# Depthwise 3x3 taps as diagonal matmuls, value copies on another engine, and a new set of due times

## The chip, the cores and the metric

The kernel runs on one core of a Trainium2 chip. A core has five engines that run their own instruction queues side by side: TensorE (PE in the profile), which multiplies matrices and writes to the accumulators (PSUM); VectorE (DVE); ScalarE (ACT); GpSimd (POOL); and SyncE (SP), which here only issues transfers. DMA engines move data between the chip's memory and the core's. The metric is the device time of one execution in microseconds (us). Before the change, three runs took 5207.44, 5217.47 and 5219.44 us: the median is 5217.47.

## What is computed

The input is a batch of 8 images of 256 channels and 32x32 pixels, fp32. Four layers follow, each adding a function of the group-normalised input to its input:

```
x = x + L0(gn(x))   # attention, 8 heads of 64, q and k normalised
x = x + L1(gn(x))   # 3x3 convolution, 256 -> 256 channels
x = x + L2(gn(x))   # 3x3 convolution, 256 -> 256 channels
x = x + L3(gn(x))   # the mixer, below
```

The mixer (layer 3), cut to its steps:

```
xn = layernorm(xs, norm_w, norm_b)
xm = mamba_v(four groups of 64 channels of xn) + skip_scale * xc      # selective scans over 1024 tokens
g  = sigmoid(conv1d(conv1d(x_concat, qdw), qpw));  xg = g * xm
R  = conv1d(conv1d(xg, rdw, groups=C), rpw) + xg
xm2 = conv1d(conv1d(concat(xs, R), fdw, groups=2C), fpw) + xs
x_local  = conv1d(xm2, lc_w, groups=C)
x_global = mha(xm2, 8 heads of 32)
x_out = gelu(layernorm(concat(x_local, x_global) @ fc_w.T + fc_b))
xi = ln_hw(x_out as image)
xi = conv2d(xi, dwc_w, 3x3, padding 1, feature_group_count=C) + dwc_b   # depthwise: one 3x3 filter a channel
out = layernorm(xi, norm_w, norm_b) @ proj_w.T + proj_b
```

The line with `dwc_w` is the one whose work moves: each pixel of a channel is the sum of nine neighbours, each with its own weight.

## The kernel before

Tiles have 128 channels (partitions) by 1024 pixels; an image is two such halves, t = 0 and 1. The whole program is first recorded, operation by operation, in streams: for each image b, `A` (layer 0's attention), `O` (its output projection), `C` (both convolutions), `N` (the load and norm ahead of the scans), `F0` to `F3` (what each of the four scans needs), `S` (the scan steps), `Z0` to `Z3` (what follows each scan), `B` (mixer up to its attention and with it) and `E` (the mixer's back end). `V` makes the convolutions' weights once.

A planner then writes the order of every engine out by hand. The table `PACE` has, for each stream and image, four due times between which the stream's operations are spread (`rank`, line 489); `arrange` (line 522) goes through them by a model of the engines, picks among the operations that could begin earliest the one with the lowest rank, and each engine is given its instructions in that fixed order. So an engine that waits at an instruction holds up all that stands behind it. Due times matter only by the order in which they put operations. An operation that needs nothing but constants (`fetches`, line 459) is due no earlier than its first user.

Buffers come from pools, and the planner gives a pool's tiles out in turn: `wsp` has 6 tiles `w` of 128x512 for weights, which ACT's queue loads (`chunk`, line 831); `ps_big` has 2 accumulator tiles `big` of 128x1024; `ps_cv` 2 and `ps_acc` 1 of 128x512; `hsp` 4 tiles `hs` of 128x1024 for the scans; `vp` one tile `v`, shared by the values of layer 0's attention and the mixer's.

What the steps of the prediction touch:

- *The scan* (`scan_steps`, line 1674) has 64 units an image. A unit is, on DVE, `hs <- du*bc` (drive), two scans `hs <- da, hs` whose decays `da` ACT makes, and `hs <- hs*bc` (weigh). After each pair of units PE adds up: four matmuls `y <- hs, sel`. These free the two `hs` tiles. 
- *Around the scan*: `branch_front` (line 1587) has the matmuls `raw,w`, `u,w_mxpw` and `u,mdtw`; `branch_back` (line 1649) has `xm,w_minw` and `u,w_moutw`, and the addition that ends `xm`.
- *The mixer up to its attention* (`back_layers`, line 1958): matmuls `xm,qdw`, then `q,qpr`, the gate, `rd,w`, `fd,w`, and `x`; then `mixer_attention` (line 1818). Its values tile has, for each of 8 heads, 32 columns of values and 32 of ones (the ones give the softmax sums). DVE fills the ones with a memset over 128x2048 elements and copies the values from the accumulator twice (128x1024 each).
- *The back end* (`back_out`, line 2114, and `back_end`, line 2129): a projection into `room[0]` and `room[1]`; a layer norm, which has 16 pairs of one-column matmuls (`mean_w`), a chain of 12 small DVE instructions (the inverse root) and 8 matmuls `ident,ln_r`; a GELU; statistics of each channel; then per half one activation that normalises `xo[t]`, one that makes the centre tap, and eight `scalar_tensor_tensor` on DVE, one for each other tap. Half 1 of the result goes to `room[0]`, the tile that half 0 of the input is in. A second layer norm (first `room,mean_w`, 4 matmuls, then as above) and the projection `room,w` (8 matmuls) end the image.

The tap loop of a half:

```
scalar.activation(dw[t], xo[t], AF.Identity, bias=col("dwc_b", t), scale=col("dwc_w", 9 * t + 4))
for k in (0, 1, 2, 3, 5, 6, 7, 8):
    rows, from_rows = inside(k // 3 - 1)
    at, from_at = inside(k % 3 - 1)
    vector.scalar_tensor_tensor(acc[:, rows, at], src[:, from_rows, from_at],
        col("dwc_w", 9 * t + k), acc[:, rows, at], ALU.mult, ALU.add)
```

Every instruction goes through one recording line, so the profile gives all of them line 252; they are told apart by their tiles' names. An fp32 matmul shows as two records of PE and two of PEld (its weight loads).

Of the kernel before, what the change touches and what calls it, by code (L numbers as in the profile page):

```python
# [36 lines left out]
OUT_OF_TURN = {("ps_big", "big")}  # L37
PACE = {
    "A": (
        (415, 603, 929, 929),  # L40
        (1475, 1542, 1636, 1677),
        (1977, 2062, 2145, 2236),
        (2549, 2617, 2690, 2765),
        (3076, 3147, 3224, 3283),
        (3606, 3674, 3747, 3821),
        (4137, 4220, 4311, 4396),
        (4656, 4723, 4796, 4870),
    ),
    "B": (
        (2311, 2384, 2458, 2526),  # L50
        (2865, 2923, 2982, 3036),
        (3355, 3425, 3503, 3574),
        (3852, 3881, 4047, 4098),
        (4408, 4491, 4580, 4659),
        (4945, 5041, 5139, 5255),
        (5504, 5504, 5512, 5512),
        (6342, 6379, 6547, 6547),
    ),
    "C": (
        (1149, 1194, 1496, 1509),  # L60
        (1208, 1832, 1921, 2046),
        (2224, 2341, 2469, 2597),
        (2762, 2875, 3002, 3127),
        (3255, 3395, 3538, 3671),
        (3884, 3987, 4058, 4187),
        (4323, 4456, 4598, 4744),
        (4735, 4944, 5116, 5233),
    ),
    "E": (
        (2525, 2566, 2613, 2646),  # L70
        (3084, 3103, 3136, 3171),
        (3588, 3631, 3669, 3706),
        (4120, 4150, 4198, 4218),
        (4644, 4694, 4725, 4759),
        (5008, 5022, 5022, 5044),
        (5557, 5647, 5741, 5758),
        (5720, 5815, 5874, 5959),
    ),
    "F0": (
        (1525, 1563, 1607, 1611),  # L80
        (1772, 1776, 1816, 1954),
        (1459, 1509, 1529, 1529),
        (1904, 2029, 2038, 2039),
        (2248, 2334, 2334, 2334),
        (2815, 2815, 2904, 2904),
        (3595, 3601, 3609, 3609),
        (3315, 3520, 3761, 3761),
    ),
    "F1": (
        (1577, 1590, 1645, 1653),  # L90
        (2262, 2311, 2312, 2316),
        (2734, 2754, 2782, 2817),
        (3328, 3348, 3375, 3411),
        (3776, 3788, 3814, 3856),
        (4420, 4421, 4428, 4443),
        (4824, 4844, 4869, 4884),
        (5274, 5355, 5414, 5468),
    ),
    "F2": (
        (1730, 1776, 1802, 1811),  # L100
        (2088, 2268, 2292, 2387),
        (2836, 2854, 2873, 2921),
        (3363, 3396, 3401, 3411),
        (3922, 3927, 3928, 3958),
        (4159, 4364, 4376, 4487),
        (4918, 4945, 4994, 4997),
        (5538, 5541, 5541, 5558),
    ),
    "F3": (
        (1920, 1924, 1930, 1993),  # L110
        (2476, 2476, 2480, 2525),
        (3002, 3013, 3022, 3041),
        (3501, 3501, 3502, 3598),
        (4012, 4030, 4080, 4100),
        (4622, 4624, 4692, 4692),
        (5082, 5106, 5106, 5106),
        (5660, 5662, 5662, 5666),
    ),
    "N": (
        (1199, 1199, 1199, 1199),  # L120
        (2025, 2026, 2048, 2106),
        (2336, 2342, 2408, 2423),
        (2960, 3081, 3112, 3112),
        (3129, 3130, 3174, 3174),
        (3403, 3699, 3729, 3736),
        (4640, 4640, 4690, 4740),
        (4647, 4673, 4674, 4771),
    ),
    "O": (
        (1255, 1264, 1264, 1264),  # L130
        (1734, 1735, 1744, 1774),
        (2235, 2283, 2300, 2310),
        (2777, 2777, 2779, 2779),
        (3324, 3339, 3359, 3361),
        (3834, 3866, 3866, 3874),
        (4391, 4425, 4425, 4425),
        (4897, 4897, 4897, 4922),
    ),
    "S": (
        (1620, 1839, 2008, 2139),  # L140
        (2183, 2391, 2531, 2706),
        (2703, 2914, 3059, 3230),
        (3221, 3433, 3574, 3750),
        (3759, 3977, 4120, 4292),
        (4299, 4511, 4647, 4810),
        (4819, 5033, 5203, 5349),
        (5830, 5830, 5853, 5853),
    ),
    "V": (
        (1265, 1502, 1519, 1531),  # L150
    ),
    "Z0": (
        (1761, 1774, 1792, 1798),
        (2279, 2279, 2306, 2312),
        (2808, 2830, 2853, 2868),
        (3347, 3358, 3565, 3568),
        (3887, 3898, 3921, 3944),
        (4101, 4114, 4136, 4235),
        (4933, 4933, 4973, 4986),
        (5530, 5535, 5536, 5543),  # L160
    ),
    "Z1": (
        (1730, 1768, 1774, 1842),
        (2364, 2382, 2385, 2439),
        (2873, 2924, 2956, 2972),
        (3404, 3437, 3450, 3491),
        (3995, 4009, 4040, 4052),
        (4490, 4501, 4528, 4570),
        (5033, 5038, 5045, 5091),
        (5550, 5559, 5561, 5561),  # L170
    ),
    "Z2": (
        (1943, 1944, 1944, 1951),
        (2535, 2535, 2539, 2556),
        (3047, 3047, 3048, 3052),
        (3557, 3557, 3562, 3575),
        (4149, 4149, 4151, 4157),
        (4515, 4515, 4518, 4561),
        (5153, 5154, 5154, 5166),
        (5902, 5902, 5902, 5902),  # L180
    ),
    "Z3": (
        (2042, 2074, 2103, 2103),
        (2667, 2697, 2699, 2704),
        (3215, 3238, 3340, 3345),
        (3746, 3746, 3765, 3798),
        (4287, 4299, 4306, 4312),
        (4806, 4806, 4806, 4809),
        (5266, 5280, 5394, 5394),
        (5760, 5760, 5862, 5862),  # L190
    ),
    "H": (
        (-1268, -1255, -985, -985),
        (-819, -819, -762, -762),
        (-1453, -1453, -1438, -1185),
        (-657, -469, -357, -354),
        (-155, -155, -155, -155),
        (213, 213, 437, 463),
        (244, 542, 565, 602),
        (714, 714, 733, 843),  # L200
    ),
}

# [255 lines left out]
def appraise(ops, groups, rooms):  # L459
    for g in groups:  # L460
        op = ops[g.ops[0]]
        g.locks, g.bytes = locks(op), 0.0
        if g.tiles and all(region(a)[0] not in rooms or in_dram(a) for a in op["ins"]):
            if op["name"] == "dma_start" and in_dram(op["ins"][0]):
                g.fetches = not in_dram(op["outs"][0])
            elif op["name"] == "memset":
                g.fetches = True
        if g.engine:
            g.holds, g.takes = cost(op)
            if op["name"] == "dma_start":  # L470
                g.queue = True
                g.bytes = 4 * max(
                    int(np.prod([k for _, k in a.ap])) for a in op["outs"] + op["ins"]
                )
            elif g.engine == 2:
                g.table = TABLES.get(op["func"], 7)
            continue
        g.holds, beside = 0.0, set()
        for op in (ops[n] for n in g.ops):
            n = elements(op["outs"][0])  # L480
            if op["array"] != (P, P) and n > P and beside and op["at"] not in beside:
                beside.add(op["at"])
                continue
            beside = {op["at"]}
            g.holds += max(n / 0.6, 215 if g.holds else 135) + STAGGER[op["array"]]
        g.takes = g.holds + 165
# [262 lines left out]
def preact_stack(ctx: ExitStack, tc: tile.TileContext, I, out, cols):  # L749
# [1068 lines left out]
    def mixer_attention(x2, img, exact=False):  # L1818


        v = vp.tile([P, NKT, 8, 64], F32, tag="v", name="v3")
        vector.memset(v[:, :, :, 32:64], 1.0)
        wv = chunk("ainv", 0)
        for kt in range(0, NKT, 4):
            ps = big_tile()
            for i in range(4):
                for c in range(2):
# [4 lines left out]
                        start=c == 0,  # L1832
                        stop=c == 1,
                    )
            vector.tensor_copy(
                v[:, kt : kt + 4, :, 0:32],
                ps.rearrange("p (k a b) -> p k a b", k=4, b=32),
            )
# [285 lines left out]
    def inside(shift):  # L2124

        at = slice(max(0, -shift), 32 - max(0, shift))
        return at, slice(at.start + shift, at.stop + shift)

    def back_end(img, out_b):
        xo = room[0:2]  # L2130
        sq = [room[2], work("ln_sq")[:, 0:N]]
# [17 lines left out]
        for t in range(2):  # L2149
# [4 lines left out]
                bias=shift[:, t : t + 1],  # L2154
                scale=rs[:, t : t + 1],
            )
            src, acc = image(xo[t]), image(dw[t])
            scalar.activation(
                dw[t],
                xo[t],  # L2160
                AF.Identity,
                bias=col("dwc_b", t),
                scale=col("dwc_w", 9 * t + 4),
            )
            for k in (0, 1, 2, 3, 5, 6, 7, 8):
                rows, from_rows = inside(k // 3 - 1)
                at, from_at = inside(k % 3 - 1)
                vector.scalar_tensor_tensor(
                    acc[:, rows, at],
                    src[:, from_rows, from_at],  # L2170
                    col("dwc_w", 9 * t + k),
                    acc[:, rows, at],
                    ALU.mult,
                    ALU.add,
                )
        sq = [room[1], work("ln_sq")[:, 0:N]]
        layer_norm(dw, sq, WHOLE, big_tile, affine("norm_w", "norm_b"))

# [173 lines left out]
```

## Time and profile before

| what | value |
|---|---|
| runs before (us) | 5207.44, 5217.47, 5219.44 |
| median | 5217.47 |
| the profiled execution's own time | 5205.82 |
| its span, first to last instruction | 5204.1 |
| mean granted clock of TensorE | 0.941 |
| PE, DVE, ACT, POOL busy | 4700.7, 4115.6, 2880.8, 3.3 |
| DMA read and written | 483.18 MB, 63.18 MB |

The profile is one execution. "Busy" is the time in which an engine had at least one instruction at work. A granted clock of 1.00 is TensorE's full speed; at 0.50 it works at half. In a row of a group of instructions stand the engine, the operation, the tiles written and read, the shape, the count, then the busy time in us and the mean of one in ns, and last the idle time of the engine just before them with what ended it. In a timeline a row begins with its start and length in us. [...]

The longest chain of work through the span goes through PE for 64% of it and through DVE for 23%; the matmuls that write the `big` tile alone take 36% of it, and the scan's `hs` instructions on DVE 13%.

### The profile page before, as it was taken

The page shows a single profiled execution, that of the slowest core. Times are in us where ns is not written, and L with a number is a line of the kernel's source. Part 1 is how long each engine was busy: PE and PEld are TensorE (multiplying, and loading weights), DVE is VectorE, ACT ScalarE, POOL GpSimd, SP SyncE. Part 2 cuts the span into 40 slices and gives each one's busy share as a digit, 9 for nine tenths or more (in the row PEclk, how much of TensorE's full clock was granted, in tenths as well). Part 3 has the DMA queues.
Part 4 walks back from the last instruction along what each step waited for, and adds up shares of the span by engine and source line. Part 5 has one row for each costly group of instructions (what it writes and reads, how often), then busy time and mean ns, then how long its engine had stood idle before and what let it go on. Part 6 is the DMA issues. An engine that isn't in the chain of part 4 may idle for free.

```text
span 5204.1 us, 53545 instructions
## 1 busy us (share of the span) xinstructions
PE 4700.7 (90%) x18998; PEld 1917.1 (37%) x18998; DVE 4115.6 (79%) x5650; ACT 2880.8 (55%) x3768; POOL 3.3 (0%) x18
## 2 busy tenths in 40 slices
PE   8999879989999999999999999999999899698595
PEld 3363243243432534244442444325343343232222
DVE  3335989888888968979897788888877989999903
ACT  4426445646665565646666555655656556566342
POOL 0000000000000000000000000000000000000000
PEclk9999889999999999999999999899999999798696
DMA  4133344344343433433423343324433444344100
GB/s 134 46 100 110 121 151 127 95 125 134 106 125 101 144 100 108 126 102 126 131 91 107 106 142 125 112 74 141 123 109 108 125 131 157 98 126 126 66 18 23
DMA packets 256658, 575.15 MB, mean 111 GB/s; under 512 B 51192, under 2 KB 79224, under 8 KB 256384
## 3 DMA queue, kind: packets, MB, share of 16 engines
q1 hardware_dynamic: 167680, 431.11, 26.5%
q10 hardware_dynamic: 88704, 140.55, 8.8%
q8 instruction: 152, 2.49, 0.2%
q14 instruction: 122, 1.00, 0.1%
HBM read 483.18 MB, written 63.18 MB: 105 GB/s over the span
## 4 chain that ended last, share of the span: by engine, by line
PE 64%; DVE 23%; ACT 5%; issue 4%; DMA 3%; SPq 1%; DVEq 0%; ACTq 0%
PE big L252 36%; PE cv L252 14%; DVE hs L252 13%; PE acc L252 12%; PE y L252 2%; ACT p L252 2%; DVE room L252 2%; DMA rs<-inv 1%; DVE xt L252 1%; DVE u L252 1%; DVE st L252 1%; DVE xm L252 1%; SPq L252 1%; DVE p L252 1%; ACT taps L252 1%
## 5 line engine op out<-in xcount | busy, mean ns | idle before, releaser
L252 ACT ACTIVATE p<-big 128x1024 f32<-128x1024 f32 x1024 | 1013.4, 1019 | 556.1 <-PE big L252 487.7
L252 ACT ACTIVATE da<-dt,a_neg 128x512 f32<-128x512 f32 x1024 | 727.8, 720 | 721.6 <-DVE hs L252 584.8
L252 PE MATMUL acc<-p,v 128*64 128x512 f32 x3072 | 827.8, 622 | 31.3 <-ACT p L252 28.3
L252 PE MATMUL cv<-taps,w 128*128 128x256 f32 x3072 | 746.0, 393 | 40.3 <-DVE taps L252 29.4
L252 PEld LDWEIGHTS cv<-taps,w 128*128 128x128 f32 x3072 | 580.3, 194 | 295.6 <-issue 147.2
L252 DVE TENSOR_TENSOR hs<-du,bc 128x1024 f32<-128x1024 f32 x512 | 613.4, 1210 | 73.7 <-PE y L252 61.1
L252 DVE TENSOR_TENSOR_SCAN hs<-da,carry,hs 128x512 f32<-128x512 f32 x512 | 638.1, 1271 | 9.1 <-ACT da L252 8.2
L252 DVE TENSOR_TENSOR hs<-hs,bc 128x1024 f32<-128x1024 f32 x512 | 621.7, 1214 | 18.2 <-ACT carry L252 16.6
L252 PE MATMUL big<-q,k 64*128 64x512 f32 x2048 | 586.3, 654 | 31.3 <-ACT p L252 23.0
L252 DVE TENSOR_TENSOR_SCAN hs<-da,hs 128x512 f32<-128x512 f32 x512 | 608.9, 1210 | 5.0 <-ACT da L252 3.5
L252 DVE TENSOR_TENSOR p<-p 128x1024 f32<-128x1024 f32 x256 | 311.8, 1218 | 227.6 <-ACT p L252 164.7
L252 PE MATMUL y<-hs,sel 128*32 128x512 f32 x2048 | 336.9, 643 | 121.2 <-DVE hs L252 119.3
L252 PEld LDWEIGHTS acc<-p,v 128*64 128x64 f32 x3072 | 161.3, 136 | 590.7 <-issue 415.7
L252 PEld LDWEIGHTS big<-q,k 64*128 64x128 f32 x2048 | 160.3, 189 | 427.7 <-issue 207.7
L252 PE MATMUL big<-qk,qk 32*128 32x512 f32 x2048 | 298.1, 645 | 3.1 <-ACT qk L252 2.2
L252 PE MATMUL cv<-p,v 128*64 128x512 f32 x1024 | 276.9, 612 | 0.0
L252 PE MATMUL big<-xn,w 128*128 128x512 f32 x512 | 232.8, 600 | 2.8 <-ACT v L252 2.5
L252 PE MATMUL big<-o,w 128*128 128x512 f32 x384 | 182.5, 621 | 12.5 <-DVE o L252 12.2
L252 PEld LDWEIGHTS y<-hs,sel 128*32 128x32 f32 x2048 | 50.1, 111 | 337.8 <-DVE hs L252 187.6
L252 DVE SCALAR_TENSOR_TENSOR room<-room,vec,room 128x992 f32<-128x992 f32 (+1 forms) x128 | 156.7, 1224 | 10.0 <-ACT room L252 9.2
L252 PEld LDWEIGHTS big<-qk,qk 32*128 32x128 f32 x2048 | 82.3, 184 | 187.2 <-issue 140.1
L252 PEld LDWEIGHTS big<-xn,w 128*128 128x128 f32 x512 | 94.0, 190 | 130.0 <-issue 115.2
(234 smaller groups left out, 5038.5 us busy)
## 6 DMA issues: line engine op xcount, KB each, us to landing
bc<-bc SPq DMA_DIRECT2D x256, 512.0 KB
w<-wc ACTq DMA_DIRECT2D x384, 256.0 KB
dt<-dt_m SPq DMA_DIRECT2D x128, 512.0 KB
du<-du_m SPq DMA_DIRECT2D x128, 512.0 KB
rs<-inv SPq DMA_DIRECT2D x64, 256.0 KB
raw<-xm SPq DMA_DIRECT2D x64, 256.0 KB
dt_m<-dt SPq DMA_DIRECT2D x128, 128.0 KB
du_m<-a SPq DMA_DIRECT2D x128, 128.0 KB
```

Source lines behind the costliest of these rows:

```text
L252: made = op["call"](*args, **kwargs).ins
```

## The change

Five things change.

1. In `back_end`, the depthwise taps of images 5 and 6 (both halves) and of half 1 of image 7 are done by TensorE. ACT makes nine diagonal matrices of 128x128 for a half, `ident` scaled by the tap's weight of each channel, in three `w` tiles; 18 matmuls (nine taps, two halves of 16 rows, cut at the image's edge) add up in a `big` tile; ACT brings the sum out with the bias. The other images, and half 0 of image 7, keep the loop on DVE.
2. The mixer's memset of ones goes from DVE to POOL.
3. The mixer's values are copied out of the accumulator by ACT, not by DVE.
4. An activation that reads only constants counts as a fetch, so that the diagonals are due no earlier than their first user.
5. All numbers of `PACE` are set anew. The row `H` is used by no stream, before or after.

```diff
 PACE = {
     "A": (
-        (415, 603, 929, 929),
-        (1475, 1542, 1636, 1677),
...
+        (-682, -424, -117, -25),
+        (516, 618, 694, 732),
...
     "E": (
...
-        (5008, 5022, 5022, 5044),
-        (5557, 5647, 5741, 5758),
-        (5720, 5815, 5874, 5959),
+        (3976, 3978, 4015, 4017),
+        (4691, 4842, 5048, 5087),
+        (4451, 4453, 4775, 4871),
...
     "S": (
...
-        (4819, 5033, 5203, 5349),
-        (5830, 5830, 5853, 5853),
+        (3878, 4092, 4264, 4402),
+        (4841, 4852, 4853, 4853),
...
-            elif op["name"] == "memset":
+            elif op["name"] in ("memset", "activation"):
                 g.fetches = True
...
-        vector.memset(v[:, :, :, 32:64], 1.0)
+        pool.memset(v[:, :, :, 32:64], 1.0)
...
-            vector.tensor_copy(
+            scalar.copy(
                 v[:, kt : kt + 4, :, 0:32],
                 ps.rearrange("p (k a b) -> p k a b", k=4, b=32),
             )
...
+    def shifts():
+        for k in (4, 0, 1, 2, 3, 5, 6, 7, 8):
+            yield (k, *inside(k // 3 - 1), *inside(k % 3 - 1))
+
+    def taps_on_vector(x, dw, t):
...
+    def taps_on_array(x, dw, t):
+
+        diagonals = []
+        for n, (k, *_) in enumerate(shifts()):
+            if n % 4 == 0:
+                w = wsp.tile([P, HALF], F32, tag="w", name="w")
+            diagonals.append(w[:, (n % 4) * P : (n % 4 + 1) * P])
+            scalar.activation(
+                diagonals[n], ident, AF.Copy, scale=col("dwc_w", 9 * t + k)
+            )
+        src, ps = image(x), big_tile()
+        acc = image(ps)
+        for n, (k, rows, from_rows, at, from_at) in enumerate(shifts()):
+            for half in range(2):
+                first, last = max(rows.start, half * 16), min(rows.stop, half * 16 + 16)
+                shift = from_rows.start - rows.start
+                tensor.matmul(
+                    acc[:, first:last, at],
+                    diagonals[n],
+                    src[:, first + shift : last + shift, from_at],
+                    start=n == 0,
+                    stop=n == 8,
+                )
+        scalar.activation(dw, ps, AF.Identity, bias=col("dwc_b", t))
...
-            src, acc = image(xo[t]), image(dw[t])
...
+            if img["at"] in (5, 6) or (img["at"], t) == (7, 1):
+                taps_on_array(xo[t], dw[t], t)
+            else:
+                taps_on_vector(xo[t], dw[t], t)
```

`taps_on_vector` is the loop shown above, as a function.

## The prediction

> **What bounds the kernel now.** The page first: shares, then where in the span they hold.
>
> ```profile
> PE 4700.7 (90%) x18998; PEld 1917.1 (37%) x18998; DVE 4115.6 (79%) x5650; ACT 2880.8 (55%) x3768; POOL 3.3 (0%) x18
> ...
> PE   8999879989999999999999999999999899698595
> ...
> DVE  3335989888888968979897788888877989999903
> ...
> PEclk9999889999999999999999999899999999798696
> ```
>
> PE is near full for 34 slices of 130 us; in the last six it is not, while DVE is. So two regimes: PE bounds the first 4400 us, with 285 us idle in all (4400 less PE's busy time in 22 windows of 200 us); the tail is bound by something else. Stage windows of the tail (start:end, length, then PE, PEld, DVE, ACT, POOL busy, granted clock, DMA share, GB/s):
>
> ```profile
> 4400.00:4480.00 80.00, 60.13 (x233) 27.04 (x232) 75.19 (x108) 45.12 (x53) 0.00 (x0) 0.80 0.43 127
> 4480.00:4530.00 50.00, 29.18 (x79) 12.01 (x80) 48.49 (x45) 26.91 (x32) 0.00 (x0) 0.70 0.30 77
> 4530.00:4580.00 50.00, 41.61 (x102) 17.33 (x105) 45.67 (x63) 21.49 (x27) 0.00 (x0) 0.89 0.40 132
> 4580.00:4800.00 220.00, 188.71 (x839) 55.95 (x831) 218.13 (x198) 152.43 (x200) 0.00 (x0) 0.93 0.42 130
> 4800.00:4905.00 105.00, 47.54 (x147) 18.18 (x150) 102.60 (x119) 35.07 (x49) 0.00 (x0) 0.55 0.16 51
> ...
> 5100.00:5204.00 104.00, 51.67 (x152) 30.85 (x152) 41.20 (x70) 17.28 (x15) 0.00 (x0) 0.63 0.06 23
> ```
>
> From 4400 to 4905, where image 7's scan ends (its last y matmuls are at 4905), DVE works 490 of 505 us and PE 367. After it comes image 7's mixer, then its back end from 5100, a chain in which both engines wait for each other. What DVE does in 4400 to 4905 besides the scan, by groups of DVE instructions in that window:
>
> ```profile
> L252 DVE SCALAR_TENSOR_TENSOR room<-room,vec,room 128x992 f32<-128x992 f32 x16 | 19.8, 1238 | 0.1
> L252 DVE SCALAR_TENSOR_TENSOR room<-room,vec,room 128x961 f32<-128x961 f32 x16 | 19.3, 1208 | 3.7 <-ACT room L252 3.6
> ...
> L252 DVE MEMSET v<- 128x2048 f32 x2 | 3.5, 1765 | 0.8 <-issue 0.8
> ```
>
> These 32 multiply-adds are the taps of images 5 and 6: 39 us of DVE in the stretch that DVE bounds. Image 7's 16 stand alone, in the timeline of the end:
>
> ```profile
> 5104.36 0.19 PEld L252 LDWEIGHTS big<-local,w 128*128 128x128 f32 x1 [0.24 <-issue]
> 5104.79 0.19 PEld L252 LDWEIGHTS big<-local,w 128*128 128x128 f32 x1 [0.24 <-issue]
> ...
> 5140.91 10.13 DVE L252 SCALAR_TENSOR_TENSOR room<-room,vec,room 128x961 f32<-128x961 f32 x8 [3.63 <-ACT room L252]
> 5151.14 1.24 ACT L252 ACTIVATE room<-room,vec 128x1024 f32<-128x1024 f32 x1 [10.26 <-DVE room L252]
> ...
> 5152.41 10.13 DVE L252 SCALAR_TENSOR_TENSOR room<-room,vec,room 128x961 f32<-128x961 f32 x8 [1.37 <-ACT room L252]
> 5162.66 0.50 PEld L252 LDWEIGHTS big<-room,mean_w 128*128 128x128 f32 x2 [11.00 <-issue]
> 5162.69 5.46 PE L252 MATMUL big<-room,mean_w 128*128 128x512 f32 x6 [9.45 <-DVE room L252]
> ```
>
> Two channel halves of 8 taps run one after the other, PE idle beside them. Also to read: at 5104 a weight load starts every 0.43 us, two per fp32 matmul of 512 columns; so one takes 0.86 us. The six records at 5162 take twice that.
>
> **The change, part by part.** *Price of a half on PE.* Nine shifted copies, cut at the image's edge, are 1024 + 4x992 + 4x961 = 8836 columns in 18 matmuls: 8836/512 x 0.86 = 14.8 us, 29.6 for an image, 74 for all five halves. DVE loses 40 taps x 1.22 = 49 us. ACT gains 45 diagonals of 128x128; no such row, so between ACT's 128x64 exponential (0.26) and the 128x512 one with a column scale (0.72): 0.34 by a line between 17 elements (0.23) and 512, 3 us a half. ACT is busy 281 of 505 us there and the diagonals wait for no data but a weight buffer, so I cost them at nothing; uncovered they would be 15 us. The evacuation (1.1) replaces the first tap's activation (1.24).
>
> *Mixer values.* Per image DVE loses a memset (1.77) and two copies (1.21 each), ACT gains two copies (its own 128x1024 row: 1.01), POOL a memset (0.95 for 1028 columns, so about 1.9); nothing is queued behind it on POOL. In images 0 to 5 the copies lie beside a full PE. The memset sits where DVE is full and PE starves (4075 to 4125: DVE 49.7, PE 31 of 50). I take 6 x 1.77 = -10 us; bounds 0 and 6 x 4.2 = -25.
>
> [...]
>
> *Paces.* The numbers are shifted by about a thousand everywhere; only the order they give counts. I set the instruction orders of both programs beside each other and gave each instruction its row's mean, scaled to the engine's busy total. PE work ahead of the first y of images 0 to 7: before 449, 877, 1416, 2001, 2628, 3176, 3810, 4219; after 448, 868, 1417, 2002, 2609, 3166, 3807, 4264. Up to image 6 they differ by under 20 us, so I take 0 for the paces, bounds +-20.
>
> *Images 5 and 6, to the end of image 7's scan.* From image 5's norm (4479) on, DVE had 415 us of work to the scan's last instruction and took 426 (97%). In the new order it has 373: less 36 for taps (in the scan's pitch), 4 for values, the rest image 6's second norm, moved behind the scan. At 97% that is 383. But the new order of PE puts all 36 of image 5's matmuls ahead of image 7's first y: 29.6 + about 2 for a cold clock, from 4479 to 4511; then w_moutw, mean, raw, qdw, sixteen small pairs, w_mxpw, 17 us of rows and about 4 of waits: first y near 4532. Four hs buffers let DVE do four units (18.8) meanwhile, and 8.6 of other things: 27.4 of 53, so 25.6 us idle. 383 + 26 = 408 against 426: **-18**. Image 6's 36 matmuls lie between the scan's last y groups; DVE has 37 us left there and PE needs 30 + 5 for y + 2 cold: **+3** for the overhang. Bounds: no stall, -44; taps at half clock throughout, +28 and +22 more.
>
> The diagonals of an image fill all six w buffers, so the next weight loads (rpw, fpw, projw), issued on ACT's queue, wait until its matmuls are done, and the scan's decays can stand behind them. The trace has this wait already: ACT reaches da late behind w loads 7 times, 29 us in all. I take 0, since DVE stalls at image 5 anyway and ACT is busy 35 of 105 us at image 6; two such waits would be +8.
>
> *After the scan.* Image 6's second norm and projection now stand in PE's queue among image 7's qdw, qpr and rd. Before, the projection's 8 matmuls (6.9) stood there too, but ahead of qpr; now they come after it, behind a norm that waits for DVE and ACT. By rows rd starts 34.5 us after the last y against 26.8 before: **+8**, bounds 0 and +14. Its two loads and two stores on SP (0.34 us of issue each) go with it, onto a queue that no longer feeds a scan: 0, and 1.4 if all stood in the way.
>
> *The last back end.* Half 1 starts on PE at 5139.7, when its activation ends, beside DVE's half 0. PE has been idle for 10 us, thus cold: at 5100.3 it took 3.6 us to double its pace, at 5162.7 it had not in 5.5. So 14.8 + 1.8 to 2.7, and the evacuation: done at 5158 instead of 5162.5. The three mean matmuls left then run warm, 2.6 for 5.46: **-7** together; at half clock throughout +8.
>
> [...]
>
> **Sum:** -10 -18 +3 +8 -7 = -24. The profiled execution took 5205.8 us (span 5204.1 and 1.7 around), so 5182; the runs' median lies 11.7 above it: 5193.
>
> **Rivals.**
> (a) *Full relief.* DVE does not stall behind image 5's matmuls and image 6's remnants are hidden: -42 at the scan's end, -10, -7: -59, 5158. For it: PE is idle 21 of 50 us in 4480 to 4530. Against: PE's order puts y behind all 36.
> (b) *Hidden anyway.* The mixer of image 6 in 4580 to 4800, with PE at 189 of 220 us, sets the pace, and the stall eats the rest: 5217 +-12. Against: DVE is at 218 of 220 there.
> (c) *Slower: taps at half clock.* One mechanism: PE is granted 0.55 in 4800 to 4905 and 0.5 at 5162; if short gaps keep it there, 36 taps cost 59 us. Image 5's stall grows by 28, image 6's overhang by 22, the last half by 15: -24 + 65 = +41, 5258. It breaks even where these 74 us of matmuls are granted about 0.75. For it: in both places PE was starved before. Against: 32 us back to back is long against the 3.6 us seen.
>
> **How the numbers follow.** Forecast 0.52 (its own range 5172 to 5212), a 0.18, b 0.17, c 0.13. About 0.3% (16 us) is what a measurement tells from no change: below 5202 faster, above 5233 slower. Faster: 0.47 of the forecast + 0.18 + 0.02 of b = 0.67; slower 0.13; same 0.20. From 5146 to 5230 leaves out a third of a and most of c, under 0.2.
>
> **What would show it.** DVE idle of about 25 us near 4500, waiting for PE; first y of image 7 some 30 us later than before; DVE busy over 95% from there to the scan's end, 15 to 20 us earlier than 4905; tap matmuls at 0.43 us a record after the first 4 us; image 7's rd later behind its last y; 97 us rather than 104 from the last mixer to the end. Wrong if the first 4400 us move by over 20 us, if no such stall appears, or if the tap records stay at 0.86.

## The result, and the profile after

| | median (us) | lowest to highest | runs |
|---|---|---|---|
| before | 5216.43 | 5207.44 to 5219.44 | 4 |
| after | 5151.43 | 5147.77 to 5153.91 | 4 |

The ratio is 0.9876, with a 95% interval of 0.9863 to 0.9889: the change takes 65 us off, and 24 were predicted. The profiled execution of after has a span of 5151.1 us against 5204.1, so 53 of the 65 us can be looked for in the traces.

The page of the changed kernel, busy time and slices:

```profile
PE 4757.1 (92%) x19178; PEld 1946.1 (38%) x19178; DVE 4037.5 (78%) x5586; ACT 2911.2 (57%) x3829; POOL 17.8 (0%) x26
...
PE   8999899999999999999999999999999899898796
...
DVE  3336989987988968889886988878878899799802
...
PEclk9999899999999999999999999999999999898897
```

PE has 56 us more to do than before and DVE 78 less, and the span is still shorter. In the slices PE's last six went from 698595 to 898796, with a higher clock beside them (798696 to 898897).

To see where the time went, the span is cut at marks that both traces have: the first scan of image 1; image 5's statistics of each channel ahead of its taps ("norm 5"); the scan's last y matmul; image 7's first `rd` matmul; image 7's norm; the end. Times in us, all from the traces; the rows below the first two are experiments told further down.

| kernel | image 1's scan at | norm 5 at | norm 5 to last y | to rd | to norm 7 | to the end | span |
|---|---|---|---|---|---|---|---|
| before | 972.7 | 4477.4 | 428.4 | 27.8 | 203.5 | 67.0 | 5204.1 |
| after | 949.4 | 4442.4 | 409.9 | 36.0 | 202.4 | 60.4 | 5151.1 |
| after, two more | 950.7, 949.5 | 4452.0, 4440.7 | 409.9, 409.9 | 36.0, 36.0 | 201.9, 201.8 | 60.6, 60.7 | 5160.4, 5149.0 |
| all taps back | 948.6 | 4449.6 | 431.4 | 46.5 | 200.5 | 65.2 | 5193.1 |
| image 5's taps back | 951.4 | 4445.4 | 420.3 | 36.0 | 202.6 | 60.2 | 5164.4 |
| image 6's taps back | 950.7 | 4441.7 | 420.3 | 46.5 | 200.7 | 60.7 | 5169.9 |
| image 7's half back | 947.5 | 4437.8 | 410.0 | 36.0 | 206.5 | 66.0 | 5156.2 |
| copies back | 948.5 | 4451.1 | 409.9 | 37.4 | 206.8 | 58.7 | 5163.9 |
| memsets back | 948.8 | 4441.9 | 408.9 | 37.4 | 201.8 | 60.7 | 5150.7 |
| values back, images 5 to 7 | 948.3 | 4442.0 | 415.2 | 37.6 | 201.9 | 59.5 | 5156.2 |
| values back, two runs | 949.2, 950.0 | 4457.5, 4462.5 | 411.1, 410.9 | 37.4, 37.4 | 206.3, 206.3 | 59.0, 58.9 | 5171.3, 5175.9 |
| taps and values back | 950.7 | 4466.6 | 435.4 | 47.3 | 202.2 | 67.0 | 5218.5 |
| before's order, values moved | 978.3 | 4487.4 | 428.7 | 27.9 | 203.7 | 67.0 | 5214.7 |

The stages behind norm 5 repeat to within 1 us between the three profiles of after, while norm 5 itself moves by 11 us. In before's order, too, two profiles agree behind norm 5 (726.7 and 727.3 us to the end) and are 10 us apart at it (the first row and the last; their work differs in the values alone). So the last four stages can be read from single profiles, and the first 4400 us only from several.

The steps of the prediction behind norm 5, in after's trace. Image 5's 72 tap records on PE start at 4444.0 and the last at 4476.3, 0.45 us each on average: the first seven 0.77 to 1.02 us, the rest near 0.42. Windows over them and the stretch behind (start:end, length, then PE, PEld, DVE, ACT, POOL busy, granted clock, DMA share, GB/s):

```profile
4425.00:4450.00 25.00, 12.20 (x37) 6.87 (x37) 18.03 (x42) 11.34 (x11) 0.00 (x0) 0.57 0.59 171
4450.00:4475.00 25.00, 25.00 (x62) 11.59 (x61) 17.93 (x16) 6.94 (x13) 0.00 (x0) 1.00 0.14 42
4475.00:4500.00 25.00, 25.00 (x97) 12.25 (x99) 8.96 (x20) 9.29 (x9) 0.00 (x0) 0.86 0.30 97
4500.00:4525.00 25.00, 21.09 (x53) 8.31 (x46) 24.32 (x30) 16.97 (x18) 0.00 (x0) 1.00 0.43 145
...
4580.00:4750.00 170.00, 141.20 (x624) 35.86 (x623) 168.31 (x155) 125.84 (x177) 1.80 (x1) 0.92 0.41 128
4750.00:4800.00 50.00, 34.16 (x114) 15.88 (x112) 48.53 (x58) 24.04 (x36) 0.00 (x0) 0.74 0.28 89
4800.00:4852.00 52.00, 41.65 (x110) 14.52 (x114) 51.53 (x59) 18.00 (x26) 0.00 (x0) 0.79 0.28 91
```

From 4450 on, behind their seventh record, the taps run at a full clock (1.00 in the second row; from 4444 to 4450 it is 0.50), and DVE stands idle beside them and behind them: 7.1 + 16.0 us in the second and third rows. From 4500 it is full again: 48.53 of 50 and 51.53 of 52 us in the last two rows, up to the scan's end. The first y of image 7 comes 51.9 us after norm 5, against 26.0 before. The stall that was predicted at "25.6 us idle" is there, though not all of it is a wait for PE: of DVE's waits from 4440 to 4530, PE ended 13.1 us and ACT 12.8. The taps of image 6 and of image 7's half run alike: from the sixth or seventh record on some 0.42 us each.

The last half, in the timeline of after's end (start, length):

```profile
5093.38 17.65 PE L252 MATMUL big<-room,w 128*128 128x512 f32 x36 [10.89 <-ACT room L252]
5094.49 10.13 DVE L252 SCALAR_TENSOR_TENSOR room<-room,vec,room 128x961 f32<-128x961 f32 x8 [3.63 <-ACT room L252]
5110.87 1.02 PE L252 MATMUL big<-room,mean_w 128*128 128x512 f32 x2
5111.12 1.11 ACT L252 ACTIVATE room<-big,vec 128x1024 f32<-128x1024 f32 x1 [16.66 <-PE big L252]
5112.28 2.84 PE L252 MATMUL big<-room,mean_w 128*128 128x512 f32 x6 [0.40 <-ACT room L252]
```

Half 1 takes PE 17.65 us beside DVE's 10.13 for half 0, and the six mean records behind it 2.84, where they took 5.46.

The two mixer steps and the diagonals, by groups of instructions (busy, mean ns):

```profile
L252 ACT ACTIVATE w<-ident,vec 128x128 f32<-128x128 f32 x18 | 6.5, 392 | 0.0
...
L252 ACT COPY v<-big 128x1024 f32<-128x1024 f32 x2 | 2.0, 1013 | 1.9 <-PE big L252 1.9
```

```profile
L252 POOL MEMSET v<- 128x2048 f32 x8 | 14.4, 1806 | 4708.7 <-PE acc L252 4015.1 <-PE cv L252 693.6
```

The prices were 0.34, 1.01 and 1.9 us; they are 0.39, 1.01 and 1.81. Image 5's diagonals are done by 4418, before its taps begin, so the taps do not wait for them. All eight memsets on POOL took 1.80 or 1.81 us, nearly as long as on DVE (1.77), also the one in 4580 to 4750, where DVE was busy 168 of 170 us.

### The profile page after: what moved, and what is told of

It is laid out like the page before. It is cut to its first block, busy times and chain, and to the rows that moved or that the text cites. A ratio compares the mean times of both kernels' runs of the same rounds, so it can differ in the third digit from the quotient of the medians.

```text
span 5151.1 us, 53923 instructions
## 1 busy us (share of the span) xinstructions
PE 4757.1 (92%) x19178; PEld 1946.1 (38%) x19178; DVE 4037.5 (78%) x5586; ACT 2911.2 (57%) x3829; POOL 17.8 (0%) x26
## 3 DMA queue, kind: packets, MB, share of 16 engines
q14 instruction: 124, 1.02, 0.1%
## 4 chain that ended last, share of the span: by engine, by line
PE 66%; DVE 20%; ACT 6%; DMA 4%; issue 3%; SPq 1%; ACTq 0%; DVEq 0%
PE big L252 38%; PE cv L252 14%; PE acc L252 12%; DVE hs L252 11%; PE y L252 3%; ACT p L252 2%; DVE room L252 1%; DVE xt L252 1%; DVE p L252 1%; DVE u L252 1%; DMA rs<-inv 1%; SPq L252 1%; DVE st L252 1%; ACT taps L252 1%; DMA du<-du_m 1%
## 5 line engine op out<-in xcount | busy, mean ns | idle before, releaser
L252 PE MATMUL y<-hs,sel 128*32 128x512 f32 x2048 | 312.7, 627 | 62.7 <-DVE hs L252 52.0
L252 PE MATMUL big<-room,w 128*128 128x512 f32 (+3 forms) x308 | 145.0, 625 | 29.1 <-ACT room L252 28.5
L252 DVE RECIPROCAL few_inv<-few 128x16 f32<-128x16 f32 (+1 forms) x48 | 13.4, 279 | 168.7 <-DMA few<-sums 168.2
```

The source lines that it names most:

```text
L252: made = op["call"](*args, **kwargs).ins
```

## The experiments

A new order comes with every change of the operations, since the planner sorts them anew. So the decisive experiments keep an order as it is: the planner is given the one program, and the instruction that is issued at a place is another. All were run beside the kernel before on the same chip; "ratio" is to it.

**1. Paces or values?** Before with after's paces only, and before with the values moved (memset to POOL, copies to ACT) and planned anew with its own paces:

```diff
     "A": (
-        (415, 603, 929, 929),
+        (-682, -424, -117, -25),
...
```

and, in the second,

```diff
-        vector.memset(v[:, :, :, 32:64], 1.0)
+        pool.memset(v[:, :, :, 32:64], 1.0)
...
-            vector.tensor_copy(
+            scalar.copy(
```

> The kernel before with the new PACE table and nothing else of the change. After gained 53 us of span, 35 of them before the back end of image 5 starts (its norm at 4442 against 4477 us), where 10 were predicted. Theory P (the new order of the earlier images brings most of those 35): image 5's norm 20 to 30 us earlier than before, the whole 15 to 30 us faster (5187 to 5202). Theory V (the values taken off DVE bring them): norm within 10 us of before, the whole within 12 us of before (5204 to 5228).

> The kernel before, with the memset of ones on POOL and the value copies on ACT, planned anew with the old PACE. Theory V: image 5's norm 25 to 40 us earlier than before, the whole 25 to 45 us faster (5172 to 5192). Theory P: norm about 10 us earlier, the whole about 10 to 15 us faster (5202 to 5207), the prediction's own price.

Measured: 5308.22 us, ratio 1.0196 (1.0176 to 1.0216), and 5272.3 us, 1.0125 (1.0108 to 1.0142). Both are slower. The first has image 1's first scan 23 us early, as in after, and then loses from image 2 on (+22 to +78 us at the first scans); the second loses 34 us at image 3. Neither says what a part is worth: a set of paces fits the operations that it was made for, and another program under it gets an order that costs 60 to 96 us. This is why the rest keeps orders.

**2. Values, order kept.** First before's order with the values on ACT and POOL, then after's order with the values back on DVE:

```diff
-        pool.memset(v[:, :, :, 32:64], 1.0)
+        plan.instead(
+            ("Pool", "memset"), ("DVE", nc.vector.memset), v[:, :, :, 32:64], 1.0
+        )
...
-            scalar.copy(
+            plan.instead(
+                ("Activation", "copy"),
+                ("DVE", nc.vector.tensor_copy),
```

> As the run before, but the order of the kernel before is kept as it stands: only the 8 memsets and 16 copies are issued on POOL and ACT at their old places in it. The prediction's price is 10 us (bounds 0 and 25) up to image 5 and some 4 after it: 5202 or so. Theory V: 30 us or more up to image 5. Theory P: 5 to 15 us.

> The changed kernel with its order kept as it stands, but the 8 memsets and 16 copies issued on DVE at the same places. Theory V: loses most of the 35 us up to image 5, the whole 25 to 45 us slower than the changed kernel (5177 to 5197). Theory P: 8 to 15 us slower (5160 to 5167).

Measured: 5208.93 us, ratio 0.999 (0.9978 to 1.0002), so in before's order the values are worth nothing that can be told; and 5177.04 us, 0.9945 (0.9927 to 0.9963), 25 us over after. The same saving is worth nothing in one order and some 25 us in the other.

**3. Taps, order kept.** After's order with the taps back on DVE, all eight of a half in one block, at the place where the sum came out of the accumulator:

```diff
                 taps_on_array(xo[t], dw[t], t)
+                if plan.recording and img["at"] in (5,):
+                    end = len(plan.ops)
+                    taps_on_vector(xo[t], dw[t], t)
+                    now = [(o["engine"], o["call"], *o["args"]) for o in plan.ops[end:]]
+                    del plan.ops[end:]
+                    for o in plan.ops[first:]:
+                        o["instead"] = []
+                    plan.ops[-1]["instead"] = now
```

> The changed kernel with its order kept, only the taps of image 5 back on VectorE, all at the place in the order where the sum came out of the accumulator. Theory of the prediction (PE's 36 matmuls make DVE stand still for some 25 us, and DVE is the bound to image 7's scan end): DVE gets back 16 x 1.22 = 19.5 us of work and loses the stall, so image 7's last scan is 0 to 6 us earlier than in the changed kernel and the time is 5145 to 5152. Rival (the relief of DVE counts here, the stall is slack that something else fills): 15 to 20 us later, 5166 to 5171.

> The same for the taps of image 6 alone. Theory of the prediction: in the last 100 us of image 7's scan DVE is the bound and PE is half idle; DVE gets 19.5 us more, so the scan ends 15 to 20 us later than in the changed kernel and the time is 5166 to 5172. Rival (image 6's matmuls hold up the y matmuls as much as they relieve DVE): within 5 us of 5151.

> The same for half 1 of image 7 alone. Theory of the prediction: the two halves run one after the other on DVE again and the three mean matmuls behind them are cold again: +7 us, 5156 to 5161. Rival (half 1 on PE is as long as the two halves on DVE were): within 3 us of 5151.

> All five halves back on VectorE, order kept: what the taps are worth in this order as a whole. Theory of the prediction: the sum of the three, -3 + 17 + 7 = +21 us, 5168 to 5177. If the taps were what made the gain larger than predicted, it would be 5190 and more; if the paces and the values made nearly all of it, 5160 and less.

Measured, with before at 5208.54 on this chip: 5171.3 (0.993, 0.9913 to 0.9946), 5174.37 (0.9941, 0.9923 to 0.9958), 5160.42 (0.9906, 0.9889 to 0.9922) and 5188.12 us (0.9958, 0.9941 to 0.9975). The medians carry the unsteady first 4400 us; the stages behind norm 5 tell the taps apart. Image 5's cost 10.4 us, all ahead of the last y. Image 6's cost 10.4 there and 10.5 more ahead of rd, since the image's second norm, which stands in PE's queue ahead of rd, is then later too. Image 7's half costs 5.3 to 5.6 behind norm 7 (and 4 ahead of it, where no tap is; the values' runs show the same step, and its cause stays open). All together cost 743.5 less 708.7, 34.8 us from norm 5 to the end.

That image 5's taps were worth 10 us contradicts the theory of the prediction. What PE waits for most from 4440 to 4530, first in after, then with image 5's taps back:

```profile
PE big L252 <- ACT room L252: 10.5, 1, 10.5
PE big L252 <- DVE r L252: 2.3, 2, 1.7
```

```profile
PE big L254 <- DVE room L254: 34.5, 2, 21.4
PE big L254 <- DVE u L254: 15.2, 1, 15.2
```

And the same run's windows:

```profile
4450.00:4475.00 25.00, 5.69 (x6) 1.25 (x6) 23.78 (x22) 6.48 (x12) 0.00 (x0) 0.50 0.17 62
4475.00:4500.00 25.00, 8.26 (x13) 3.66 (x14) 19.26 (x18) 4.90 (x8) 0.00 (x0) 0.55 0.24 74
4500.00:4525.00 25.00, 24.32 (x101) 11.78 (x100) 16.27 (x33) 16.82 (x17) 0.00 (x0) 0.93 0.38 121
```

Without the 36 matmuls PE does not go on to the scan's y: it stands still (busy 5.7 and 8.3 of 25 us) until DVE has done the taps, since image 5's second norm is next in its queue. The first y of image 7 is later, not earlier (62.4 us after norm 5 instead of 51.9), and DVE still idles 15.7 us in 4450 to 4525, against 23.8 in after. The stall belongs to the order, which has image 5's whole back end ahead of that y, and not to the place of the taps. What the taps would cost on DVE if they were spread between the scan's instructions, as before's order has them, was not tried.

**4. The order alone; the norm moved; one row of paces.** After's order with values and taps both back (experiments 2 and 3 together); after with the last due times of image 6's back end later; before with the first row of every stream from after's table, laid over it:

```diff
     "E": (
-        (4691, 4842, 5048, 5087),
+        (4691, 4729, 4766, 4804, 4842, 4894, 4945, 4996, 5048, 5738, 5738, 5739, 5739),
```

and, in before,

```diff
     "A": (
-        (415, 603, 929, 929),
+        (258, 516, 823, 915),
...
```

> The changed kernel's order with the work of before: the mixer's values and all five halves of taps back on VectorE, each at the place of the instruction that it replaces. What the new order is worth by itself. If the parts add up: taps 35 us (span of all taps back, 42, less 7 of drift ahead of image 5) and values 20 to 26 are all of the gain, and the time is within 10 us of before, with 20 us gained at image 5's norm and given back behind it. If the order itself makes the gain: 5190 and less. If the new order is made for the moved work and is bad for the old: over 5225.

> The changed kernel with only the due times of the last third of image 6's back end later, so that its second norm and projection stand behind image 7's rd, within the second half of its attention; the order up to the scan's end is the same. Theory of the prediction (they hold up rd by 8 us): rd starts 27 to 28 us after the last y instead of 35.5, and as PE is busy 23 to 24 of 25 us in the attention, their 11 to 13 us of matmuls cost 3 to 11 there: image 7's norm 5 us earlier to 3 later. Rival (PE has room in the attention): image 7's norm 8 us earlier, 5143.

> Before with the due times of image 0 alone taken from the changed kernel (each stream's first row, moved by 940 us so that the two tables lie over each other). If these rows make the early gain, image 1's scan starts 20 to 25 us earlier than before (as in the changed kernel); if it takes image 1's rows too (its convolutions against image 0's scan), within 10 us of before. Whatever is gained may be lost later, since before's other rows were not set for it: 5170 to 5300.

> The changed kernel once more, for comparison on the same chip: 5140 to 5155.

The order alone: 5219.9 us, ratio 1.0002 (0.9992 to 1.0012). The new order, with the old work, gains nothing. By the table it is 11 us early at norm 5 and then gives back 7 us at the last y and 19.5 at rd, 25 in all to the end. That would make it 14 us slower, which its median isn't: before's profile lies 10.6 us under its median, and since the stages behind norm 5 repeat, most of that must lie ahead of norm 5. Against an ordinary run of before the new order is thus early by an estimated 21 to 26 us at norm 5 (the 11 us of the profiles, or 15 by the averages told below, and the 10.6), and loses them behind it.

The norm behind rd: 5168.76 us, 0.9895 (0.9878 to 0.9911), slower than after. rd does start 12.6 us earlier behind the last y (23.4 for 36.0), so the norm held it up; but the attention, from its first matmul to the sum behind its last, takes 148.0 us instead of 124.5, and loses more. Windows of 4 us through this norm:

```profile
5008.00:5012.00 4.00, 3.84 (x20) 0.77 (x19) 0.00 (x0) 3.07 (x4) 0.00 (x0) 1.00 0.21 51
5012.00:5016.00 4.00, 3.84 (x28) 2.77 (x26) 0.00 (x0) 2.23 (x3) 0.00 (x0) 0.95 0.07 17
5016.00:5020.00 4.00, 4.00 (x16) 2.66 (x16) 1.28 (x8) 0.00 (x0) 0.00 (x0) 0.50 0.19 57
5020.00:5024.00 4.00, 3.34 (x16) 3.02 (x15) 0.73 (x5) 0.00 (x0) 0.00 (x0) 0.50 0.19 74
5024.00:5028.00 4.00, 3.08 (x12) 1.30 (x11) 2.35 (x2) 1.94 (x2) 0.00 (x0) 0.77 0.00 0
5028.00:5032.00 4.00, 3.04 (x10) 0.81 (x12) 0.00 (x0) 2.25 (x3) 0.00 (x0) 0.66 0.02 4
```

The norm's 32 one-column records begin in the second window (PEld goes from 0.77 to 2.77 us there), and in the third the granted clock is 0.50 while PE is busy 4.00 of 4 us.

The first image's paces: 5299.36 us, 1.0153 (1.0136 to 1.017). Image 1's scan is 11 us early and image 2's 24 us late: which rows of the table make the early gain stays open. After once more: 5152.31 us, 0.9864 (0.9847 to 0.988). No kernel tried was faster than it beyond the noise.

**5. Which part of the values?** After's order with only the copies back on DVE, only the memsets, both but only in images 5 to 7, and both once more:

```diff
+        back = img["at"] in (5, 6, 7)
+        if back:
+            plan.instead(
+                ("Pool", "memset"), ("DVE", nc.vector.memset), v[:, :, :, 32:64], 1.0
+            )
+        else:
+            pool.memset(v[:, :, :, 32:64], 1.0)
```

> The changed kernel's order with only the values' 16 copies back on VectorE (the memsets stay on POOL). If the copies lie beside a full PE in images 0 to 5, as the prediction took it: within 5 us of the changed kernel, 5147 to 5157. If VectorE's work counts in full: 16 x 1.21 = 19 us, 5168 to 5175.

> The same with only the 8 memsets back on VectorE (the copies stay on ScalarE). By the prediction's price 6 x 1.77 = 10 us or, with images 6 and 7, 14: 5160 to 5167. If only the copies count: within 5 us of the changed kernel.

> The same with memset and copies back on VectorE in images 5, 6 and 7 alone. If the values count alike in each image, 3/8 of 25 = 9 us, 5158 to 5165; if they count only where VectorE sets the pace (images 6 and 7), nearly all of it, 5168 to 5177; if only in the first images, within 4 us of 5152.

> The changed kernel beside them on the same chip: 5145 to 5160.

> The changed kernel's order with memsets and copies back on VectorE once more. If the two add up: 10 us over the changed kernel, about 5162, ratio 0.990. If they cost more together: 5172 to 5180, ratio 0.993 to 0.9945.

| back on DVE | median (us) | ratio | interval |
|---|---|---|---|
| nothing (after) | 5152.55 | 0.9886 | 0.9864 to 0.9907 |
| memsets | 5151.25 | 0.9881 | 0.9859 to 0.9904 |
| copies | 5162.7 | 0.9900 | 0.9879 to 0.9920 |
| both, images 5 to 7 | 5159.44 | 0.9893 | 0.9874 to 0.9912 |
| both | 5173.88 | 0.9918 | 0.9903 to 0.9932 |

The memsets back cost nothing, the copies back about 10 us, both 21 by the medians and 17 by the ratios (the last row ran on another chip, beside its own before). The intervals overlap; but no run with the copies back is below 5159.28, and none of after beside it above. Whether the two cost more together than apart isn't settled. The steady stages behind norm 5 tell more: to the end they take 708.7 us in after, 708.8 with the memsets back, 712.8 with the copies, 713.4 and 713.8 with both, and 714.1 with both in images 5 to 7 alone. So the values of the last images cost some 5 us there, most of it by the copies, and the rest of the loss stands ahead of norm 5.

## Why the prediction was right or wrong

**The first 4400 us: wrong, and nearly all of the miss.** Predicted -10 for the values and "0 for the paces". One of the prediction's own signs of being wrong, that this stretch moves by over 20 us, came true. Behind norm 5 the change gave 18.0 us (726.7 less 708.7), where -18 +3 +8 -7 made 14. The other 47 of the 65 us, where 10 were predicted, lie ahead of norm 5, or between profile and median. In eight profiles with after's order and the values on ACT (after three times, the four of experiment 3, the moved norm) norm 5 comes at 4444 us on average; in three with the values on DVE at 4462; in before's one profile at 4477. So the values gave 18 and the order 15, or the estimated 21 to 26 of experiment 4 against an ordinary run. Two terms failed:

- *Values.* The step was to price the six memsets and to let the copies "lie beside a full PE". The runs turn this round: the memsets are worth nothing by themselves, the copies 10 us. The sum over all images is 21 to 25 us by the medians, where the prediction had 10 and 4 more behind norm 5. Why the copies count in this order and not in before's (0.999) is not shown.
- *Paces.* The step was to compare the work that stands on PE ahead of the first y of each image, to find it equal, and so to put the term at 0. The order's gain is there early: image 1's first scan comes at 947.5 to 951.4 us in the table's rows with after's order, against 972.7 and 978.3 in before's, and none of the moved instructions stands ahead of it (after's first such memset is at 1014 us). What the order changed was the waiting. What PE waited for in the first 4400 us (total, times, longest), in before:

```profile
PE y L252 <- DVE hs L252: 56.0, 22, 8.5
PE cv L252 <- DVE taps L252: 29.4, 12, 9.2
PE big L252 <- ACT p L252: 26.0, 19, 6.2
PE big L252 <- DVE u L252: 22.7, 7, 6.8
```

in after:

```profile
PE big L252 <- ACT p L252: 50.6, 36, 8.0
PE y L252 <- DVE hs L252: 24.9, 13, 4.4
PE cv L252 <- DVE taps L252: 17.1, 13, 6.1
...
PE big L252 <- DVE u L252: 12.3, 5, 4.9
```

and in after's order with the old work (experiment 4):

```profile
PE big L254 <- ACT p L254: 50.0, 34, 8.0
PE y L254 <- DVE hs L254: 27.6, 15, 4.7
PE cv L254 <- DVE taps L254: 16.8, 10, 6.1
...
PE big L254 <- DVE u L254: 13.2, 5, 4.9
```

Waits for DVE in these three rows fall from 108.1 to 54.3 us, and the attention's wait for ACT rises from 26.0 to 50.6. With the order alone they are 57.6 and 50.0, so this is the order's doing; of the 18 us of the values only some 3 stand in these rows. A sum of work ahead of a mark can't show such waits.

**Norm 5 to the last y: near in sum, wrong inside.** Predicted -18 and +3, measured -18.5; that the sum came near is luck. The stall was there, but it was charged to the 36 matmuls: by the prediction's own terms image 5's taps, 19.5 us off DVE and 26 of stall, would have been a loss of some 6 us. They gain 10.4, for without them the same place in PE's queue waits longer, for DVE. Taken one after the other, in this order, the parts are +7 for the new order (the back end ahead of y), -4 for the values, -21.5 for the taps: before 428.4, then 435.4, 431.4 and 409.9 in the table.

**The mixer: right.** Predicted +8 at rd, measured +8.2 (27.8 to 36.0). What was not seen is that the taps of image 6 work against it: with them on DVE it would have been 18.7.

**The last back end: right.** Predicted -7, measured -6.6; the half on PE took 17.65 us, where 16.6 to 17.5 were worked out, and the six mean records took 2.84 us at a granted clock of 1.00 (before, 5.46 at 0.50).

**From profile to median: a part of the miss.** The prediction added the 11.7 us by which before's median lay over its profile. After's profile (5152.86) is 1.4 us above its median, before's (5205.82) 10.6 under its own, so 12 of the 65 us lie between profile and median and appear in no comparison of the two traces. By the estimate of experiment 4 most of them belong to the order ahead of norm 5. Between chips before's median went from 5208.5 to 5216.7.

**What each part is worth.** In after's order, by the ratios of experiments 2 to 5, with after at 0.9875 (mean of three) and 0.001 being 5.2 us: the order alone 0 (1.0002). The values 0.0044 with the taps on DVE, 0.0043 to 0.0070 with the taps on PE: 22 to 37 us. The taps 0.0057 to 0.0084 with the values on DVE, 0.0083 with the values moved: 30 to 44 us. The paces by themselves gain nothing; they make an order in which the moved work counts: early by 11 to 15 us ahead of norm 5 against before's profile (an estimated 21 to 26 against its median), and behind norm 5, without the taps on PE, dear by 25.

**The rivals.** (a) Full relief, 5158, is nearest in time and wrong in reason: the stall did not vanish. (b) does not hold, since the stage to the last y became 18.5 us shorter. (c) does not hold: the granted clock beside image 5's taps was 0.50 for the first 6 us and 1.00 from 4450, and the records of all three groups of taps took some 0.42 us behind the first five to seven.

## What to carry to other kernels

When a change comes with a new order, the order can't be tried with the old work nor the work with the old order by planning anew: put the one instruction in the other's place and keep the order, or the planner's answer (here 60 to 96 us) hides what is measured. Equal work ahead of a mark says nothing of the waits ahead of it; read who waits for whom in both orders, or carry the whole of an engine's removed work as a bound on the gain. An engine that waits behind a burst may be waiting for the place of the burst's users in the queue: ask what stands next if the burst is taken away.

## What the runs showed of the hardware

In experiment 4 the granted clock fell in a series of one-column matmuls although the profile shows PE busy. The 32 records stand in an attention that ran at 1.00; PE is busy 3.84 and 4.00 of 4 us in the windows from 5012 to 5020, and the clock goes from 0.95 to 0.50; the windows to 5032 stay between 0.50 and 0.77. In after's last back end, a window over the last mean matmuls, the one behind it, and then one over the same series:

```profile
5109.00:5113.00 4.00, 3.60 (x10) 1.47 (x9) 0.00 (x0) 1.11 (x1) 0.00 (x0) 1.00 0.00 0
5113.00:5118.00 5.00, 2.51 (x7) 0.88 (x6) 2.35 (x2) 1.51 (x2) 0.00 (x0) 1.00 0.00 0
5118.00:5125.00 7.00, 6.22 (x30) 6.13 (x30) 0.09 (x1) 0.60 (x1) 0.00 (x0) 0.58 0.01 2
```

PE is busy 6.22 of 7 us and the clock is 0.58; but here PE was also idle for half of the 5 us before, so this series alone doesn't tell whether the idle time or the narrow matmuls go with the fall. In experiment 4 PE was busy 3.84 of 4 us in the window ahead, so it is the cleaner case. No run varies the width of the matmuls alone, so what brings the fall is not shown.
